# Attention over heads beside a layer of MLPs: how far ahead the MLPs run, and how the second halves of its tiles are issued

## The chip, the core and the metric

The kernel runs on one core of a Trainium2 chip. The core has five engines that take their instructions in program order, each from its own queue: TensorE (PE in the profile, with PEld for its weight loads), VectorE (DVE), ScalarE (ACT), GpSimd (POOL) and SyncE (SP, which issues most of the DMA transfers here). They wait for one another by semaphores. The metric is the device time of one execution in microseconds (us), and lower is better. The kernel before was timed six times: median 2488.54 us, from 2477.02 to 2491.85.

## The reference

Four transformer layers work on x, four sequences of 512 tokens and 288 channels, all float32. Each layer is attention and then an MLP, both with a normalisation, a shift and a scale ahead and a gate behind, which come from a conditioning vector per sequence. Layer 0's MLP is a mixture of four experts, two for each token. Layers 1 and 3 are plain. In layer 2 the attention runs over the 16 heads of one token, not over the tokens of a sequence:

```python
qkv = qkv.reshape(n, t, 3, H, DH)
q, k, v = (qkv[:, :, 0], qkv[:, :, 1], qkv[:, :, 2])
attn = jnp.einsum('nthd,ntkd->nthk', q * scale, k)
attn = jax.nn.softmax(attn, axis=-1)
out = jnp.einsum('nthk,ntkd->nthd', attn, v)
out = out.transpose(0, 2, 1, 3).reshape(n, t, d)
```

So each token has a 16 by 16 score matrix over vectors of 18, which the kernel computes on DVE and POOL, and the output is reshaped across tokens: a row of 288 channels that goes into the projection comes from many tokens of one head.

## The kernel before

The tokens are 16 tiles of 128, four for each of the four sequences (`B` = 4, `TB` = 4). The program is written out by a Python schedule. Time in it is counted in gaps: each piece of the main work on PE ends with a call of `gap(us)`, which may issue other work there. `gap` draws from four lists: `products` (work that needs PE and a PSUM bank), `lanes` (statistics and other work of DVE), `loads` and `spreads` (DMAs). An item has a due time in gaps and keys that must be ready; `mark(key, delay)` makes a key ready `delay` gaps later.

*Main work.* The attention of layer 1 runs in 64 steps of two gaps (`steps`, after 6 steps of lead). `INSIDE` names steps in the middle of which the whole MLP of one sequence of layer 1 is put (`early_mlp`, 512 tokens at a time); before, that is step 48, sequence 0. Six steps before the attention's end `begin_chain` starts the attention of layer 2, called the chain. Then come the other MLPs of layer 1 and those of layer 2 in halves of 256 tokens (`half_mlp`): two halves a sequence, 18 gaps a half. Each MLP of layer 2 waits, by a loop of empty gaps, until the normed rows of its sequence are ready (`ht`, 2, 1, b). Then layer 3's attention starts.

*The chain* (`attention_over_heads`). It is a generator, `stream`, which `follow` advances at each gap as far as a credit allows: every gap adds `flow["rate"]` (1.0 at first, then `RATE`), at most to 3.0, and each piece takes off the microseconds that it yields. Pieces that yield `BANK` need the one PSUM bank that a gap can give, and a `WAIT` ends a generator's turn until the next gap. A tile i goes through these steps:

- `kept(i, s)`: three products on PE for keys, values and queries (L839). Queries stay in one of two banks, the others are copied out by ACT (L848).
- `weigh(i, g)`, for four groups of four heads: a product (L857) and a sum (L863) on DVE give the scores `hs`.
- `shift(i)`: the maximum (L867) and its subtraction (L868), both on DVE. After every second tile ACT takes the Exp of two tiles (L1011).
- The second half, two tiles later: `denominators` (L889, DVE), `weighted(i, g)` on POOL (L873), `summed(i, g)` on DVE one tile later still (L885), `finish` (L897, POOL, and a DMA to scratch memory, L898).

The second half of an older tile is issued in the same loop as the first half of a newer one, `for i in range(n + 3)`, group by group.

*Beside the chain.* `beside` holds generators of two kinds for each sequence. `before(b)` normalises x for the chain. `after(b)`, started when a sequence's four tiles are finished, reads the reshaped rows back (`read`, L902), transposes (L915), projects (L922), adds to x, normalises and transposes again for the MLP of layer 2. They advance only while credit is above zero.

*Around it.* The weights of layer 3's attention (L248 to L257) are loaded by SP when the first products of layer 2's last sequence are done and the key "all spread" is marked; the chain marks it at its very end. SP issues in order, so a load that waits holds what stands behind it. Layer 1's and layer 2's MLP halves end with a copy on ACT (L1693) and two operations on POOL (L1694, L1695). In `gap`, products are issued early unless an item of the chain wants a bank.

## Time and profile before

One execution was profiled: 2483.05 us, of which the trace spans 2481.3 us; the mean granted TensorE clock is 0.943. The stages on PE, read from first and last instructions:

| stretch | from, us | to, us |
|---|---|---|
| one MLP of layer 1 inside its attention (L1596 to the last update) | 1232.2 | 1285.4 |
| first weigh of tile 0 to the last sum of tile 15 | 1366.7 | 1769.0 |
| first half MLP of layer 1 to the last half of layer 2 | 1366.7 | 1940.4 |
| attention of layer 3 and its MLPs | 1941.1 | 2481.3 |

| engine | busy over the span, us | share |
|---|---|---|
| PE | 2279.9 | 92% |
| DVE | 1087.0 | 44% |
| ACT | 833.0 | 34% |
| POOL | 528.3 | 21% |

The operations of the chain, by their rows:

| operation | engine, line | count | mean ns |
|---|---|---|---|
| product for the scores | DVE L857 | 64 | 1346 |
| sum over it | DVE L863 | 64 | 1353 |
| maximum | DVE L867 | 16 | 411 |
| subtraction | DVE L868 | 16 | 2089 |
| product with the values | POOL L873 | 64 | 3194 |
| sum over it | DVE L885 | 64 | 1332 |
| division by the denominator | POOL L897 | 16 | 759 |

A row of the slices is one engine over 40 equal parts of the span (62 us each), a digit being its busy share in tenths. In a row of the windows the stretch is followed by its length and then, for each engine, busy time and number of instructions, the granted clock, the share of the DMA engines and GB/s. In a row of a timeline the start and the length come first; the brackets at its end give the idle time of the engine before it and what ended it. For a line of code the least, median and largest duration in ns are given.

### The profile page before, as it was taken

The numbers are of one execution on the slowest core, as the hardware profiler recorded it, in microseconds if no ns is written. First come the engines' busy times: TensorE is split into PE (matmuls) and PEld (weight loads), VectorE is DVE, ScalarE is ACT, GpSimd is POOL, SyncE is SP. The second block draws the span as 40 slices with busy tenths as digits, with TensorE's granted clock in tenths as the row PEclk, the third lists the DMA queues.
The fourth block names the chain that finished last, engine by engine and source line by source line (L and its number), as shares of the span: only waits on it lengthen the run. The fifth ranks groups of instructions, "written<-read, shape, count | busy, mean of one in ns | idle before, by whom it ended". The sixth has DMA issues, their size and how long they took to land. (4 is left out here: it accounts for less than half of the span.)

```text
span 2481.3 us, 30149 instructions
## 1 busy us (share of the span) xinstructions
PE 2279.9 (92%) x11188; PEld 1210.4 (49%) x11188; DVE 1087.0 (44%) x1955; ACT 833.0 (34%) x1233; POOL 528.3 (21%) x544
## 2 busy tenths in 40 slices
PE   5999999799998999999999999778589999999998
PEld 2333333367775773333353677455456433333455
DVE  3556657240021025555424668989210455555100
ACT  1444444222221223344325233323223244444311
POOL 2000022120022111100010257778721100011000
PEclk8899999899999997899999899888799799999999
DMA  3311120355554541000000001100110000000000
GB/s 80 100 55 39 50 86 27 97 179 177 175 156 152 170 126 58 13 14 15 28 21 1 22 3 35 33 17 17 23 56 2 28 16 16 14 13 6 1 19 20
DMA packets 163033, 134.23 MB, mean 54 GB/s; under 512 B 81365, under 2 KB 146725, under 8 KB 162886
## 3 DMA queue, kind: packets, MB, share of 16 engines
q1 hardware_dynamic: 159520, 122.39, 16.9%
q0 software_dynamic: 3072, 9.44, 1.2%
q8 instruction: 89, 1.46, 0.2%
q14 instruction: 58, 0.48, 0.1%
q10 hardware_dynamic: 294, 0.47, 0.1%
HBM read 90.67 MB, written 26.25 MB: 47 GB/s over the span
## 5 line engine op out<-in xcount | busy, mean ns | idle before, releaser
L668 DVE TENSOR_REDUCE mx<-banks 128x1 f32<-128x512 f32 x696 | 448.2, 686 | 369.0 <-PE banks L616 367.2
L616 PE MATMUL banks<-qk 32*128 32x512 f32 x3072 | 542.8, 672 | 25.1 <-DMA qk<-qc 13.6
L661 ACT ACTIVATE ex<-banks 128x1024 f32<-128x1024 f32 x348 | 356.4, 1024 | 508.0 <-PE banks L616 499.9
L616 PEld LDWEIGHTS banks<-qk 32*128 32x128 f32 x3072 | 175.8, 191 | 240.0 <-DVE mx L668 95.3
L873 POOL TENSOR_TENSOR pv<-hs,qk 128x1152 f32<-128x1152 f32 x64 | 203.7, 3194 | 50.1 <-DVE ho L885 35.0
L690 PE MATMUL banks<-ex,va 128*32 128x512 f32 x1536 | 213.0, 626 | 0.0
L562 PE MATMUL banks<-ht,wqk 96*128 96x512 f32 (+1 forms) x360 | 189.7, 635 | 1.4 <-POOL wqk L284 0.8
L1472 PE MATMUL banks<-w_b,hid_b 128*128 128x288 f32 x684 | 189.5, 420 | 0.0
L1660 PE MATMUL banks<-ht,w 128*128 128x256 f32 x504 | 134.2, 401 | 38.4 <-ACT hid L1671 37.9
L1452 PE MATMUL banks<-block,w_b 128*128 128x256 f32 x684 | 165.4, 387 | 2.4 <-DMA w_b<-in_w 1.7
L710 POOL COPY rec<-r 128x512 f32<-128x512 f32 x48 | 29.6, 617 | 646.0 <-DVE r L706 572.3
L1464 ACT ACTIVATE hid_b<-banks,b_b 128x256 f32<-128x256 f32 x171 | 68.8, 473 | 246.1 <-PE banks L1458 144.3
L1682 PE MATMUL banks<-w,hid 128*128 128x288 f32 x504 | 151.4, 436 | 0.0
L1472 PEld LDWEIGHTS banks<-w_b,hid_b 128*128 128x128 f32 x684 | 125.1, 192 | 52.3 <-issue 24.4
L1452 PEld LDWEIGHTS banks<-block,w_b 128*128 128x128 f32 x684 | 129.4, 193 | 28.3 <-issue 8.2
L1660 PEld LDWEIGHTS banks<-ht,w 128*128 128x128 f32 x504 | 98.7, 201 | 62.0 <-ACT hid L1671 42.2
L727 PE MATMUL banks<-wp,ot 128*128 128x288 f32 x384 | 118.9, 435 | 5.9 <-DVE upd_a L522 3.5
L523 POOL TENSOR_TENSOR x<-x,upd_a 128x288 f32<-128x288 f32 x48 | 38.1, 794 | 364.2 <-DVE upd_a L522 341.6
L1682 PEld LDWEIGHTS banks<-w,hid 128*128 128x128 f32 x504 | 93.0, 197 | 45.8 <-issue 25.7
L562 PEld LDWEIGHTS banks<-ht,wqk 96*128 96x128 f32 (+1 forms) x360 | 61.6, 192 | 103.0 <-issue 89.1
L727 PEld LDWEIGHTS banks<-wp,ot 128*128 128x128 f32 x384 | 68.4, 194 | 75.2 <-issue 51.2
L690 PEld LDWEIGHTS banks<-ex,va 128*32 128x32 f32 x1536 | 31.1, 109 | 151.7 <-issue 149.9
(224 smaller groups left out, 2571.0 us busy)
## 6 DMA issues: line engine op xcount, KB each, us to landing
w_b<-in_w SPq DMA_DIRECT2D x57, 432.0 KB
w_b<-in_w SPq DMA_DIRECT2D x57, 384.0 KB
qk<-qc SPq DMA_DIRECT2D x327, 38.0 KB
wa<-in_wada SPq DMA_DIRECT2D x7, 864.0 KB
block<-x_mem SPq DMA_DIRECT2D x19, 288.0 KB
y_mem<-y_b SPq DMA_DIRECT2D x19, 288.0 KB
x_mem<-zeros SPq DMA_DIRECT2D x7, 768.0 KB
y_mem<-zeros SPq DMA_DIRECT2D x7, 768.0 KB
```

The costliest lines, as they stand in the source:

```text
L562: nc.tensor.matmul(to, st(rows, k), mv(rows, k), start=k == 0, stop=k == NK - 1)
L616: nc.tensor.matmul(to, qk[u][r, of, c * P : (c + 1) * P], qk[u][r, 1 - of, :], start=True, stop=True)
L661: nc.scalar.activation(e, WEIGHTS, AF.Exp)
L668: nc.vector.tensor_reduce(mxs[mu % 2][:, mc, h : h + 1], pm[j], AX.X, ALU.max)
L690: nc.tensor.matmul(SUMS[j * HP : (j + 1) * HP, :], vas[0][:, c, at : at + HP], ex[step, j // 2][:, j % 2, :], start=c == 0, stop=c == TB - 1,)
L727: nc.tensor.matmul(pp, done[b * NG + g][:, t * P : (t + 1) * P], w["wp"][:, g, :], start=g == 0, stop=g == NG - 1)
L873: nc.gpsimd.tensor_tensor(prod, sc[i][:, hs, :].unsqueeze(2).to_broadcast([P, GH, HD, NH]), qkv[i][:, 1].rearrange("p h d -> p d h").unsqu ...
L1452: nc.tensor.matmul(banks[:, UP + j, :BT], w1[:, k, j * P : (j + 1) * P], hx[i][:, k, :], start=k == 0, stop=False)
L1464: nc.scalar.activation(t, banks[:, UP + j, :BT], AF.Gelu_apprx_tanh, bias=b1[:, f : f + 1])
L1472: nc.tensor.matmul(banks[:, PY + t, :C], hid[j][:, t * P : (t + 1) * P], w2[:, j, :], start=f == 0, stop=f == NF - 1)
L1660: nc.tensor.matmul(banks[:, UP + j, :BT], full[:, k, (f % 3) * P : (f % 3 + 1) * P], h[:, k, s], start=k == 0, stop=False,)
L1682: nc.tensor.matmul(banks[:, PY + t, :C], hf[:, t * P : (t + 1) * P], w["w2"][f // 3][:, f % 3, :], start=False, stop=f == NF - 1,)
```

## The change

One more sequence's whole MLP of layer 1 is put inside its attention (steps 44 and 56, sequences 0 and 1), so four halves instead of six follow. `RATE` goes from 1.1 to 1.6. The subtraction of the maximum goes to POOL. The second halves are no longer issued by the tile loop's index but by their own counters (`at`): each weigh is followed by one `second()`, which issues one `weighted` and the `summed` that is two pieces behind; Exp for two tiles is issued one weigh into the tile after them. For the last two tiles every other `weighted`, and for the last tile the division, goes to DVE. Products for the next tile no longer hold the stream until they are possible. Items of `beside` that want a bank come first, and the others advance at least one piece a gap whatever the credit. The scores get four buffers instead of three; three empty gaps are put into the normalisations that ACT applies. The load of layer 3's attention weights no longer waits for the chain's end. Layer 2's MLPs also wait for their gate and count their due times anew. The normed rows behind the chain's projections may follow four gaps after them instead of six.

```diff
@@ -48,8 +48,8 @@
 N_BLOCKS = 2 * B * S // BT + NE - 1
-INSIDE = (48,)
-RATE = 1.1
+INSIDE = (44, 56)
+RATE = 1.6
 EARLY = 4
@@ -139,7 +139,7 @@
         before = flow["turn"]
-        wanted = any(item[1] for item in chain)
+        wanted = any(item[1] for item in chain + beside)
         fill(products, open_product, 0.0 if wanted else us)
@@ -172,12 +172,14 @@
-        for item in list(chain):
+        for item in beside + chain:
             if item[1]:
...
         for item in list(beside):
-            while flow["credit"] > 0 and piece(item):
-                pass
+            if not item[1]:
+                go_on = piece(item)
+                while go_on and flow["credit"] > 0:
+                    go_on = piece(item)
         for item in list(chain):
@@ -451,6 +453,8 @@
             nc.gpsimd.tensor_scalar_mul(off, off, -1.0)
+            for _ in range(3):
+                yield WAIT
         else:
@@ -778,7 +782,8 @@
         if l > 0:
-            task(loads, at_step(-LEAD) - 20, [("first products", prev, B - 1), ("all spread", prev)], load_attention(l))
+            spread_all = [] if prev == OVER_HEADS else [("all spread", prev)]
+            task(loads, at_step(-LEAD) - 20, [("first products", prev, B - 1)] + spread_all, load_attention(l))
             task(loads, at_step(-LEAD) - 20, [("x", prev, 1, B - 1)], load_projection(l))
@@ -852,7 +857,7 @@
             if g == 0:
-                sc[i] = work.tile([P, NH, NH], F32, tag="hs", bufs=3, name=f"hs_{l}_{i}")
+                sc[i] = work.tile([P, NH, NH], F32, tag="hs", bufs=4, name=f"hs_{l}_{i}")
             prod = work.tile([P, GH, NH, HD], F32, tag="va", bufs=1, name=f"pq_{l}_{i}_{g}")
@@ -865,12 +870,14 @@
             nc.vector.tensor_reduce(top, sc[i], AX.X, ALU.max)
-            nc.vector.tensor_tensor(sc[i], sc[i], top.to_broadcast([P, NH, NH]), ALU.subtract)
+            nc.gpsimd.tensor_tensor(sc[i], sc[i], top.to_broadcast([P, NH, NH]), ALU.subtract)
...
             prod = work.tile([P, GH, HD, NH], F32, tag="ex", bufs=4, name=f"pv_{l}_{i}_{g}")
-            nc.gpsimd.tensor_tensor(
+            engine = nc.vector if i >= len(tiles) - 2 and g % 2 else nc.gpsimd
+            engine.tensor_tensor(
                 prod,
@@ -894,7 +901,8 @@
             den = o.pop(("den", i))
-            nc.gpsimd.tensor_tensor(o[i], o[i], den.to_broadcast([P, NH, HD]), ALU.mult)
+            engine = nc.vector if i == len(tiles) - 1 else nc.gpsimd
+            engine.tensor_tensor(o[i], o[i], den.to_broadcast([P, NH, HD]), ALU.mult)
             nc.sync.dma_start(scratch[b][:, t * P : (t + 1) * P, :].rearrange("h t d -> t h d"), o[i])
@@ -963,7 +971,7 @@
                 yield -1.5
-            mark(("x", l, 1, b), 6)
+            mark(("x", l, 1, b), 4)
             yield from until(("x", l, 1, b))
@@ -979,41 +987,88 @@
             beside.append([before(1), False])
             yield from until(("values free", l - 1, B - 1, TB - 1))
             del ready["cleared"]
-            for i in range(n + 3):
+            at = {"shifted": 0, "weighed": 0, "weighted": 0, "summed": 0}
+            def second(behind=2):
+                k = at["weighted"]
+                cost = 0.0
+                if k < 4 * at["weighed"]:
+                    if k % 4 == 0:
+                        denominators(k // 4)
+                        cost += 0.7
+                    weighted(k // 4, k % 4)
+                    at["weighted"] += 1
+                k = at["summed"]
+                if k < at["weighted"] - behind:
+                    summed(k // 4, k % 4)
+                    at["summed"] += 1
+                    cost += 1.4
+                    if k % 4 == 3:
+                        finish(k // 4)
+                        if k // 4 % TB == TB - 1:
+                            beside.append([after(k // 4 // TB), False])
+                return cost
+            def exps():
+                for j in range(at["weighed"], at["weighed"] + 2):
+                    nc.scalar.activation(sc[j], sc[j], AF.Exp)
+                at["weighed"] += 2
+            def waiting():
+                return at["weighted"] < 4 * at["weighed"]
+            for i in range(n):
+                left = [1, 2, 0] if i + 1 < n else []
+                come = ("ht", l, 0, (i + 1) // TB)
+                def next_kept():
+                    s = left.pop(0)
+                    if s:
+                        yield BANK
+                    kept(i + 1, s)
+                    yield -1.5
                 for g in range(4):
-                    if i < n:
-                        weigh(i, g)
-                        yield 2.8
-                        if g > 0 and i + 1 < n:
-                            yield from until(("ht", l, 0, (i + 1) // TB))
-                            if g < 3:
-                                yield BANK
-                            kept(i + 1, g % 3)
-                            yield -1.5
-                    if g == 1 and 2 <= i < n + 2:
-                        denominators(i - 2)
-                        yield 0.7
-                    if i >= 3:
-                        summed(i - 3, g)
-                    if 2 <= i < n + 2:
-                        weighted(i - 2, g)
-                    yield 1.4 if i >= 3 else 0.0
-                if i >= 3:
-                    finish(i - 3)
-                    if (i - 3) % TB == TB - 1:
-                        beside.append([after((i - 3) // TB), False])
-                if i < n:
-                    shift(i)
-                    if i % TB == TB - 2:
-                        mark(("first products", l, i // TB), 1)
-                    if i % 2:
-                        for j in (i - 1, i):
-                            nc.scalar.activation(sc[j], sc[j], AF.Exp)
-                    yield 1.0
+                    weigh(i, g)
+                    yield 2.8
+                    if g > 0 and left and ready.get(come, 1 << 30) <= flow["now"]:
+                        yield from next_kept()
+                    if g == 1 and i % 2 == 0 and at["weighed"] < i:
+                        exps()
+                    if waiting():
+                        yield second()
+                shift(i)
+                if i % TB == TB - 2:
+                    mark(("first products", l, i // TB), 1)
+                at["shifted"] = i + 1
+                yield 0.4
                 if i % TB == 0 and 2 <= i // TB + 1 < B:
                     beside.append([before(i // TB + 1), False])
+                while left:
+                    if ready.get(come, 1 << 30) <= flow["now"]:
+                        yield from next_kept()
+                    elif waiting():
+                        second()
+                        yield 3.2
+                    elif at["weighed"] + 2 <= at["shifted"]:
+                        for _ in range(4):
+                            yield WAIT
+                        exps()
+                    elif at["summed"] < at["weighted"]:
+                        yield second(0)
+                    else:
+                        yield WAIT
+            while at["summed"] < 4 * n:
+                if not waiting() and at["weighed"] < n:
+                    yield WAIT
+                    yield WAIT
+                    exps()
+                second(2 if waiting() else 0)
+                yield 2.8
             mark(("over heads", l))
-            mark(("all spread", l))
             yield from clear()
         return stream()
@@ -1133,7 +1188,7 @@
                 arenas.append(
-                    work.tile([P, NH, NH], F32, tag="hs", bufs=3, name=f"arena{len(arenas)}").rearrange("p a b -> p (a b)")
+                    work.tile([P, NH, NH], F32, tag="hs", bufs=4, name=f"arena{len(arenas)}").rearrange("p a b -> p (a b)")
                 )
@@ -1832,8 +1887,9 @@
     for b in range(B):
-        while ready.get(("ht", 2, 1, b), 1 << 30) > flow["now"]:
+        while any(ready.get(key, 1 << 30) > flow["now"] for key in (("ht", 2, 1, b), ("gate", 2, 1))):
             gap(0.5)
+        rebase(starts["mlp", 2] + 2 * b * MLP_GAPS)
         for half in range(2):
...
     flush(2)
```

## The prediction

> **What bounds the kernel now.** I read the page's slices first: PE is at nine tenths almost everywhere, and falls away in one stretch alone, slices 25 to 29 (1550 to 1860 us), where DVE and POOL are the busy ones. The page's groups, the table of 20 us windows and one line's durations carry the rest.
>
> Page, busy tenths in 40 slices of 62 us:
> ```profile
> PE   5999999799998999999999999778589999999998
> DVE  3556657240021025555424668989210455555100
> POOL 2000022120022111100010257778721100011000
> PEclk8899999899999997899999899888799799999999
> ```
> Windows, engine by engine (PE, PEld, DVE, ACT, POOL), then the granted clock:
> ```profile
> 1524.00:1544.00 20.00, 20.00 (x93) 14.92 (x91) 19.49 (x16) 6.23 (x13) 15.04 (x8) 1.00 0.29 60
> 1584.00:1604.00 20.00, 11.56 (x37) 8.41 (x38) 17.98 (x19) 7.80 (x14) 18.21 (x14) 0.78 0.00 0
> 1624.00:1644.00 20.00, 7.91 (x37) 5.16 (x35) 19.17 (x16) 5.02 (x8) 14.76 (x8) 0.81 0.17 37
> 1784.00:1804.00 20.00, 2.39 (x15) 1.76 (x12) 0.00 (x0) 1.55 (x2) 4.41 (x12) 0.65 0.43 73
> 1884.00:1904.00 20.00, 20.00 (x90) 14.18 (x89) 1.17 (x4) 4.47 (x10) 2.81 (x3) 1.00 0.00 1
> ```
> The stage runs from 1366.7 us (first weigh of tile 0) to 1941.1 (first score of the last attention). DVE is full from about 1484 to 1720, PE full from 1804 on, and in two places neither is: 1436 to 1455 and 1769 to 1804. The timelines of DVE, PE and the SP queue name those two:
> ```profile
> 1454.91 0.46 DVE L442 BATCH_NORM_STATS2 st<-x 128x6 f32<-128x288 f32 x1 [18.55 <-POOL x L1695]
> ```
> ```profile
> 1804.69 1.06 PE L915 MATMUL banks<-ident,rows 128*96 128x128 f32 x4 [18.31 <-DMA rows<-scratch]
> ```
> ```profile
> 1777.77 1.99 SPq L248 DMA_DIRECT2D wqk<-in_wqk  x3
> ...
> 1799.85 0.63 SPq L252 DMA_DIRECT2D wqk<-in_bqk  x1
> 1800.58 0.40 SPq L902 DMA_DIRECT2D rows<-scratch  x1
> ```
> In the first, DVE stands in order behind statistics of an x that the MLP of sequence 1 has not finished. In the second, the rows of the last sequence are issued behind a train of weight loads 22.8 us long (1777.8 to 1800.6), and PE stands behind the rows. The lines of the subtraction and of a product beside it (least, median, largest ns):
> ```profile
> L868 DVE TENSOR_TENSOR hs<-hs,ht x16: 424/2536/3324, 1389.7 to 1730.4; 128x256 f32<-128x256 f32 x16
> ```
> ```profile
> L857 DVE TENSOR_TENSOR pq<-banks,qk x64: 1294/1348/1359, 1366.7 to 1726.0; 128x1152 f32<-128x1152 f32 x64
> ```
> A subtraction of 0.42 us takes up to 3.3, about one POOL product (3.19).
>
> **The change, part by part.** *One more whole MLP ahead of the chain.* Whole MLPs of the last layer end 37.2 us apart (2366.4, 2403.6, 2440.8). After the one inside attention 1 PE idles 3.7 us, so I take 37.2 + 3.7 = 41 us of later start; ends are 37 and the 53 us that the present one lasts (1232.2 to 1285.4, other products among it). First weigh: 1366.7 + 41 = 1408. This is paid in full, as PE is busy 0.92 to 0.98 there (1116 to 1364). The two halves that it replaces leave the stage behind.
>
> *Stall at sequence 1.* Its x is now complete before the chain starts, so the 18.6 us and the 4.3 us for the next product go. Sequence 2 is late next: its MLP is 36 gaps of the first half stage, and DVE then needs it only at tile 8. Price nothing, cover four tiles of DVE.
>
> *Subtraction.* 16 x 2.09 = 33.4 us leave DVE; POOL gets 16 x about 0.68 (its 288 element product, least 0.67) = 11. Queued behind it on POOL are the products of older tiles, behind its result the two Exp on ACT, behind these the Gelu of the MLP; Exp is now issued one weigh or more later, which covers about 4 us. Starts of tiles 7 to 15 (1537.07 to 1711.38) are 21.8 us apart, and the subtractions in them average 2.4, so the period becomes 19.4 us. DVE's own rows give 4 x (1.35 + 1.35 + 1.33) + 0.41 + 0.41 + 0.25 = 17.2, with 8 x 0.62 / 4 = 1.24 of statistics 18.5: that is the lower end, 21.8 the upper (nothing gained), and I take 19.4 because its rows are of the same stretch. The fourth hs buffer removes waits of L863 for POOL, 9.1 us in five times; I leave them inside those ends.
>
> *Rate 1.6 and second halves on their own count.* A tile is worth 4 x 2.8 + 4 x 1.4 + 0.7 + 1.0 - 3 x 1.5 = 14.0 of credit now, 12.7 gaps at 1.1; after, 13.4 at 1.6, 8.4 gaps. A half MLP is 18 gaps and 20 to 22.6 us of PE (copies at 1876.6, 1899.0, 1921.8, 1940.4), so a tile carries 8.4 x 1.15 + 4.4 (its 18 products) = 14 us of PE work, some 3 more with transposes and projections: less than 19.4, so DVE keeps setting the pace and PE does less beside it than now. POOL has 4 x 3.19 + 0.76 + 0.68 + about 4 of updates = 18, close.
>
> *Chain end.* Tiles 0 and 1 have no second halves: 48.3 us now, 44 at the higher rate. Then 14 x 19.4 = 272. Weigh of tile 15 ends at 1408 + 44 + 272 = 1724 (1729 now). The tail is now 35 us (1733.7 to 1769.0), POOL products with DVE waiting. Nine second halves stay, four of the last eight products on DVE, 2.8 of credit each: 16 gaps, 20 us (ends 12 and 35). A product on DVE has no row; it lies between 1.35 (L857) and 1.35 + 3.2 (if it waits as L868 did), and I take 2.9, the middle, inside the 20. Last sum 1744, against 1769.
>
> *Handover.* The weights of the last attention no longer wait for the chain, so their train comes right after tile 14. The 18.3 us before the last rows go. But SP is in order: by count, the rows of sequence 2 are issued within one gap of the train. If the train is first, PE stands at those rows instead, up to 18.3 us; if not, nothing. I take the middle, 9. The scratch writes behind it have two tiles (39 us) of cover.
>
> *PE after the chain.* Waiting: statistics and transposes that want a bank now move each gap, not only on credit. Tile 3 is done at tile 6.6, 48 gaps after the start; about 37 more to its normed rows, 85; the four halves of layer 1 end at 72, so 13 gaps without an MLP. The new wait for the gate is covered: its row needs the end of layer 1, gap 77, and four products, 81. The chain has some 128 gaps, so 43 go to layer 2, 2.4 halves; 5.6 remain, against 4.6 at 1804.7. Now 1804.7 to 1941.1 is 136.4 us; one half more is 20: 156. The stage ends at 1744 + 9 + 156 = 1909, against 1941: 32 us. Norm's three new waits (3 gaps, 1.2 us each) are in the 37; sorting of the beside list costs nothing, it only orders issues. The 540 us behind the stage stay. The profiled execution took 2483.05 (span 2481.3): 2451. It lies 5.5 under the median of the six runs (2488.54), so 2457.
>
> **A rule against one step.** L868 reads two tensors in SBUF and waits, L857 reads one from PSUM and never does; L873 stretches only from 3.12 to 3.42. The Trainium skill, GPSIMD Engine Reference, Specifications, says that POOL's SBUF interfaces are shared with DVE and contended by DVE instructions with two SBUF inputs, which agrees with both lines; its Perfetto Trace Analysis, Optimizing Scalar/DVE Operations, warns that for this reason moving work between the two might not help. By the warning the subtraction gives nothing: that is a rival below.
>
> **Rivals.**
> *A. As worked out*, 2457, own range 2435 to 2478. Chance 0.48.
> *B. The ends fall well*: period 18.5 (13 us), train behind the rows (9), tail 12 (8), half an MLP fewer left (10): 40 more, 2417. For it: DVE is 95% busy at 21.8 us a tile, so nothing else holds it. Against: POOL at 18 of 18.5. Chance 0.20.
> *C. Period stays 21.8*, POOL or its port bounding: 14 x 2.4 = 34 us, 2491. For it: POOL is 18.2 of 20 busy at 1584. Against: there DVE is the one it waits for (L885, 35 us). Chance 0.14. The quoted warning ends here.
> *D. Slower: Exp behind the pool's queue.* ACT waited for the subtraction up to 14.3 us, and the Gelu and PE behind it. Should that come at each of the seven pairs, half of it on DVE's path through late products, 50 us: 2507. It decides from about 5.5 us a pair (32 / 5.5, six or seven pairs). For it: one more engine between maximum and Exp. Against: Exp is issued later than now. Chance 0.18.
>
> **Numbers.** 0.3% (7.5 us) is about what can be told from no change. Faster by more: A, B and a fifth of C, 0.71; within: most of C, 0.09; slower: D and a little of C, 0.20. The range takes B's end and C's, leaving most of D out: 2413 to 2500.
>
> **What would show it.** First weigh near 1408; no L442 wait of 18 us; subtractions on POOL under 1 us; tile starts 19.4 apart (21.8 would be C); last sum near 1744; PE's idle before L915 short, or 18 us at sequence 2; five to six upd_m copies after the chain; last attention at 1909. Wrong if tiles keep their period, or if PE still waits tens of us for the normed rows of layer 2.

## The result, and the profile after

The changed kernel takes 2471.91 us (median; 2467.11 to 2482.0), beside 2485.01 for the kernel before in the same runs: a ratio of 0.9948, 95% interval 0.9936 to 0.996. That is a gain of 0.52%, some 13 us, where the forecast had 31.5. The profiled execution took 2469.37 us (span 2467.3).

All of the comparison below goes by the stage from the first weigh of tile 0 to the first score of the last attention. The earlier layers shift its start by up to 14 us from one execution to another without any edit to them (1390.2 to 1404.7 us among the versions below with two whole MLPs ahead), so its length is the sharper reading; the ratios beside it are of whole executions. The kernel before was timed again beside each batch of experiments (medians 2477.8 to 2486.9 us), so two runs are compared by their ratios to it and not by their times.

| point | before, us | forecast | after, us |
|---|---|---|---|
| first weigh of tile 0 | 1366.7 | 1408 | 1402.4 |
| maximum of tile 15 (end of its weighing) | 1729.9 | 1724 | 1730.2 |
| last sum of tile 15 | 1769.0 | 1744 | 1801.0 |
| from there to the first score of the last attention | 172.1 | 165 | 126.6 |
| first score of the last attention | 1941.1 | 1909 | 1927.6 |
| length of the stage | 574.4 | 501 | 525.2 |

The page's slices of the kernel after, busy tenths in 40 slices of 61.7 us:

```profile
PE   5999999799998999999999898897689999999998
DVE  3455656331021015555343389669420455555100
POOL 2000022121022011100010149769441000001000
PEclk8899999899999997999999998898789799999999
```

The hole of PE is narrower than before, and it is deepest at 7 and 6, in slices 27 and 28, about 1666 to 1789 us. Three windows of the kernel after (PE, PEld, DVE, ACT, POOL; granted clock; DMA share; GB/s) show two different stretches of the chain:

```profile
1480.00:1500.00 20.00, 18.69 (x80) 13.43 (x79) 19.79 (x19) 6.42 (x13) 19.73 (x10) 1.00 0.07 7
1704.00:1724.00 20.00, 10.23 (x24) 6.31 (x24) 19.72 (x22) 3.47 (x8) 16.14 (x13) 0.59 0.26 27
1724.00:1744.00 20.00, 1.42 (x5) 1.04 (x6) 7.84 (x7) 0.30 (x1) 5.31 (x6) 0.50 0.49 70
```

In the first, DVE and POOL are both full and PE almost: what the change was read to do. In the last, little computes: PE is busy 1.4 of 20 us, DVE 7.8, and the granted clock is 0.50. PE's timeline and the SP queue's name it:

```profile
1742.58 1.09 PE L923 MATMUL banks<-ident,rows 128*96 128x128 f32 x4 [28.09 <-DMA rows<-scratch]
```
```profile
1714.46 0.36 SPq L906 DMA_DIRECT2D scratch<-ho  x1
1714.91 1.98 SPq L250 DMA_DIRECT2D wqk<-in_wqk  x3
...
1737.39 0.63 SPq L254 DMA_DIRECT2D wqk<-in_bqk  x1
1738.06 0.46 SPq L910 DMA_DIRECT2D rows<-scratch  x1
```

PE comes to the transposes of sequence 2 at 1742.58 - 28.09 = 1714.5, just as the last scratch write of that sequence is issued (1714.46). Then SP issues the last attention's weight train, 23.2 us, and only at 1738.06 the read of the rows, which PE can use 4.5 us later. PE waits out the whole of it. Behind PE stand ACT and then DVE, in their own order:

```profile
1743.70 0.58 ACT L924 COPY rt<-banks 96x512 f32<-96x512 f32 x1 [30.13 <-PE banks L923]
```
```profile
1767.26 0.42 DVE L896 TENSOR_REDUCE hd<-hs 128x16 f32<-128x256 f32 x1 [35.38 <-ACT hs L1017]
```

ACT's copies for the transposed and projected rows are in front of the Exp of the last two tiles, so the second halves of those tiles begin 35 us late, and the tail is 70.8 us long (40.7 in a version below in which nothing stands at the rows). POOL, where the subtraction of tile 15 now is, stands in the same way:

```profile
1752.06 0.79 POOL L935 TENSOR_TENSOR upd_a<-upd_a,gate 128x288 f32<-128x288 f32 x1 [22.67 <-ACT upd_a L934]
...
1756.81 0.62 POOL L873 TENSOR_TENSOR hs<-hs,ht 128x256 f32<-128x256 f32 x1
```

Its maximum was there at 1730.6; the subtraction waits 26 us behind an update that waits for the rows. The duration of the subtraction is about as forecast, 0.62 us where 0.68 was taken (least, median, largest ns):

```profile
L873 POOL TENSOR_TENSOR hs<-hs,ht x16: 613/622/642, 1425.5 to 1756.8; 128x256 f32<-128x256 f32 x16
```

Over the stage, before and then after:

```profile
1366.70:1941.10 574.40, 491.53 (x2037) 344.25 (x2037) 331.24 (x376) 169.46 (x323) 310.21 (x221) 0.90 0.12 25
```
```profile
1402.40:1927.60 525.20, 445.69 (x1835) 311.74 (x1833) 310.27 (x357) 156.45 (x297) 297.86 (x223) 0.89 0.13 28
```

PE idles 574.4 - 491.5 = 83 us before and 525.2 - 445.7 = 79.5 after. The stage is 49 us shorter almost only by the work that was moved ahead of it (36 us of later start pay for that); the idle time that the change was to fill has stayed.

### The profile page after: what moved, and what is told of

Same layout as the page of the kernel before. It is cut to its first block, busy times and chain, and to the rows that moved or that the text cites. A ratio compares the mean times of both kernels' runs of the same rounds, so it can differ in the third digit from the quotient of the medians.

```text
span 2467.3 us, 30012 instructions
## 1 busy us (share of the span) xinstructions
PE 2266.4 (92%) x11134; PEld 1197.2 (49%) x11134; DVE 1069.2 (43%) x1946; ACT 832.8 (34%) x1225; POOL 520.0 (21%) x553
## 4 chain that ended last, share of the span: by engine, by line
PE 76%; DVE 8%; POOL 4%; DMA 4%; issue 2%; ACT 2%; SPq 2%; another core or an unknown queue 0%; ACTq 0%; POOLq 0%; DVEq 0%
PE banks L620 19%; PE banks L566 10%; PE banks L694 7%; PE banks L1527 7%; PE banks L1507 6%; PE banks L731 4%; PE banks L1678 4%; PE banks L1651 4%; POOL pv L880 3%; PE banks L1737 2%; PE banks L1715 2%; PE banks L1513 1%; DVE pq L862 1%; DVE mx L672 1%; DVE ho L892 1%
## 5 line engine op out<-in xcount | busy, mean ns | idle before, releaser
L620 PE MATMUL banks<-qk 32*128 32x512 f32 x3072 | 533.2, 670 | 24.8 <-DMA qk<-qc 13.5
L880 POOL TENSOR_TENSOR pv<-hs,qk 128x1152 f32<-128x1152 f32 x60 | 190.4, 3187 | 22.9 <-ACT hs L1017 22.8
L1715 PE MATMUL banks<-ht,w 128*128 128x256 f32 x432 | 117.1, 406 | 13.9 <-ACT hid L1726 13.9
L1737 PE MATMUL banks<-w,hid 128*128 128x288 f32 x432 | 128.6, 434 | 0.0
L1678 PE MATMUL banks<-w,hid 128*128 128x288 f32 x432 | 109.1, 410 | 0.0
L1715 PEld LDWEIGHTS banks<-ht,w 128*128 128x128 f32 x432 | 86.3, 205 | 33.7 <-ACT hid L1726 17.5
```

Source lines behind the costliest of these rows:

```text
L620: nc.tensor.matmul(to, qk[u][r, of, c * P : (c + 1) * P], qk[u][r, 1 - of, :], start=True, stop=True)
L880: engine.tensor_tensor(prod, sc[i][:, hs, :].unsqueeze(2).to_broadcast([P, GH, HD, NH]), qkv[i][:, 1].rearrange("p h d -> p d h").unsqueez ...
L1678: nc.tensor.matmul(banks[:, t, :C], hf[:, t * P : (t + 1) * P], w["w2"][f // 3][:, f % 3, :], start=False, stop=f == NF - 1,)
L1715: nc.tensor.matmul(banks[:, UP + j, :BT], full[:, k, (f % 3) * P : (f % 3 + 1) * P], h[:, k, s], start=k == 0, stop=False,)
L1737: nc.tensor.matmul(banks[:, PY + t, :C], hf[:, t * P : (t + 1) * P], w["w2"][f // 3][:, f % 3, :], start=False, stop=f == NF - 1,)
```

## The experiments

The theory: the idle time is at the rows. Two things put it there: the weight train ahead of the rows of sequence 2, and the three empty gaps between a read and its transposes, which PE is through before the read has landed. The rivals: the higher rate or the new order of the second halves holds the chain; the division of work between DVE and POOL does; the products at the end of the chain do. Where nothing else is said an edit is made to the kernel after.

### The train, moved

The load of the last attention waits until the rows of sequence 2 have been read:

```diff
-spread_all = [] if prev == OVER_HEADS else [("all spread", prev)]
+spread_all = [("rows read", prev, 2)] if prev == OVER_HEADS else [("all spread", prev)]
             read(b)
+            mark(("rows read", l, b), 0)
```

> The changed kernel, but the train of weight loads for the last attention is issued only once the rows of sequence 2 are issued (one added key), so it stands behind them and ahead of the rows of sequence 3. Theory T (the missing gain is the 28.1 us in which PE stands at the rows of sequence 2, priced at 9 in the prediction): PE's wait there falls to the 5 to 7 us that sequences 0 and 1 show, the Exp of the last two tiles is no longer 35 us late, and the time falls from 2472 by 19 to 28 us, to 2444 to 2453. Rival R (the stand is covered, PE being full from 1824 us on with work that only waits for the MLPs' order): under 5 us, 2467 to 2472.

Measured: 2451.89 us, ratio 0.9896 (0.9866 to 0.9925); stage 517.0 us. The kernel after is at 0.9948, so the move gives 0.52%, 13 us, less than the 19 to 28 of theory T, and the stage is 8 us shorter. PE's timeline of this kernel has what is left of the stand, and the SP queue's why:

```profile
1716.12 1.09 PE L923 MATMUL banks<-ident,rows 128*96 128x128 f32 x4 [11.14 <-DMA rows<-scratch]
```
```profile
1705.03 0.36 SPq L906 DMA_DIRECT2D scratch<-ho  x1
1711.76 0.36 SPq L910 DMA_DIRECT2D rows<-scratch  x1
1712.18 1.54 SPq L250 DMA_DIRECT2D wqk<-in_wqk  x3
```

The train is now behind the read, and still PE stands 11.1 us, where T had 5 to 7; at sequence 0 it stands 8.8 in this execution. The write to scratch memory (1705.03) must land before the read is issued, 6.7 us later; the rows are there after another 4.4. A round trip of 11 us is what the gaps were to cover (three ahead of the read and three behind it), and at this sequence PE was through all of them when the write was issued. The sums over the stage say the same, the kernel after and then this one (total, times, longest):

```profile
PE banks L923 <- DMA rows<-scratch: 40.0, 3, 28.1
```
```profile
PE banks L923 <- DMA rows<-scratch: 25.8, 3, 11.1
```

### The train, one sequence later

The same edit with sequence 3 in place of 2.

> The changed kernel with the train issued only behind the rows of sequence 3, the last. T: as the run before, 2444 to 2453, unless the last attention's first products now wait for their weights, which would show as idle time of PE ahead of L566 after 1800 us. R: 2467 to 2472.

Measured: 2460.51 us, ratio 0.9928 (0.99 to 0.9956), stage 520.4. The stand at sequence 2 is the same (11.0), and the last sequence adds one of 13.0 us. The time is in neither forecast's range, and by the ratio the version can't be told from the one above; nothing speaks for holding the train longer.

### The train, back at the chain's end

The edit of the load is undone: "all spread" is marked at the end of the chain and waited for again.

> The changed kernel with this one edit undone: the train waits for the chain's end again, and the mark is back there. T: the stand moves from sequence 2 to sequence 3; there it was 18.3 us before the change, and the chain is not held by it, so about half of the 28 us comes back: 2455 to 2465. R: 2467 to 2472.

Measured: 2478.37 us, ratio 0.9996 (0.9978 to 1.0013), stage 537.6: slower than the kernel after by 0.48%, 12 us, and no faster than the kernel before. Both forecasts missed it: T had half of the 28 us coming back. The chain does end sooner (its tail is 54 us in place of 70.8), but a stand of the same size is now at the last sequence, behind the chain:

```profile
1806.34 1.09 PE L923 MATMUL banks<-ident,rows 128*96 128x128 f32 x4 [29.56 <-DMA rows<-scratch]
```

So the load's earlier place is worth 12 us as it stands, though it only moves a stand of 28 to 30 us from one sequence to another: in this version PE still stands 10.7 us at sequence 2, without the train.

### Nine gaps in place of three

The train stays where the change has it; what moves is the distance from a read to its transposes:

```diff
             read(b)
-            for _ in range(3):
+            for _ in range(9):
                 yield WAIT
```

> After, with nine empty gaps instead of three between the read of a sequence's rows and their transposes; the train of weight loads stays where it is, ahead of the rows of sequence 2. Theory (the train delays the rows of sequence 2 by 22.8 us and the distance to their use covers only three gaps, some 10 us with the issue): nine gaps are 11 to 15 us of PE work more or less, so the stand at the rows of sequence 2 falls from 28.1 to 10 to 17 us and the short ones (6.5, 5.4) vanish; stage from first weigh to first score 495 to 512 us (after: 525; both edits together: 480), time 2440 to 2458. Rival (the distance alone does it, the train is without effect): stand under 3 us, stage within 5 us of 480, time 2425. Second rival (the train alone does it): stand over 22 us, stage over 517.

Measured: 2437.86 us, ratio 0.9816 (0.979 to 0.9841), stage 491.2: a further 1.3%, 33 us, better than the kernel after. The stand at sequence 2 is 10.4 us and the two short ones are gone, as the theory had it; stage and time are a few us better than its lower ends.

```profile
1719.97 1.09 PE L923 MATMUL banks<-ident,rows 128*96 128x128 f32 x4 [10.35 <-DMA rows<-scratch]
```

Six gaps took 17.7 us off the long stand and all of the 12 us of the short ones, 30 in all, out of a stage that is 34 us shorter. They also change the order of PE's work. In the kernel after, the transposes of sequence 0's rows (1538.59) and its four projections are issued ahead of the products of tile 8, the first of sequence 2, and DVE waits for these. With more gaps the same products come ahead of the transposes (1543.49). PE and DVE in the kernel after, then PE in the version of the next section, which has nine gaps too:

```profile
1555.59 1.62 PE L930 MATMUL banks<-wp,rt 96*128 96x288 f32 x6
1557.92 1.62 PE L844 MATMUL banks<-wqk,ht 96*128 96x288 f32 x6
1564.36 1.36 DVE L862 TENSOR_TENSOR pq<-banks,qk 128x1152 f32<-128x1152 f32 x1 [18.30 <-PE banks L844]
```
```profile
1538.29 3.08 PE L844 MATMUL banks<-wqk,ht 96*128 96x288 f32 x12
```

DVE's waits for the products of tiles 8 and 12, 18.3 and 10.9 us, are gone with nine gaps and still there (19.1 and 12.5) with the train moved alone. So the 33 us are the worth of the gaps, and how much of them is the landing of the rows and how much the order was not separated.

### Both

> The train behind the rows of sequence 2, and nine empty gaps instead of three between the issue of a sequence's rows and the first transpose that reads them. Theory T2 (what is left of the stand is PE, which is in order, meeting transposes issued too few gaps after their DMA; at rate 1.6 three gaps are about 4 us and the rows take 6 to 11 more): PE's waits at L923, 25.8 + 6.1 us with the train moved alone, fall under 5, and the stage (first weigh to first score of the last attention, 517.0 us with the train moved alone, 525.2 in the changed kernel) to about 490 to 500. Rival (the waits are only PE's slack, since layer 2's MLPs cannot start earlier anyway): stage 510 or more.

Measured: 2424.95 us, ratio 0.9752 (0.9727 to 0.9777), stage 479.5, shorter than theory T2 had. It is 2.0% below the kernel after (some 49 us), about the sum of the two edits (13 + 33). No transpose waits for rows. The windows of this kernel over the same minutes of the chain as above:

```profile
1480.00:1500.00 20.00, 18.67 (x80) 13.41 (x80) 19.79 (x18) 6.61 (x12) 19.70 (x9) 1.00 0.07 8
1704.00:1724.00 20.00, 19.42 (x82) 14.33 (x80) 16.17 (x16) 7.69 (x14) 19.84 (x13) 0.88 0.39 51
1724.00:1744.00 20.00, 15.37 (x59) 10.96 (x60) 10.29 (x9) 5.10 (x10) 19.69 (x13) 0.83 0.07 7
```

At 1480 nothing has changed; at 1704 to 1744 PE has 34.8 us of work in place of 11.7. The tail from the maximum of tile 15 to the last sum is 40.7 us in place of 70.8. Over the whole stage:

```profile
1404.66:1884.18 479.52, 435.24 (x1836) 305.36 (x1834) 304.22 (x357) 156.03 (x297) 303.50 (x223) 0.93 0.14 30
```

PE's idle time is 44.3 us, from 79.5; and its busy time falls too, by 10.5 us for the same instructions, at a granted clock of 0.93 in place of 0.89.

### Both, in the kernel before

The same two edits, and nothing of the change:

```diff
-[("first products", prev, B - 1), ("all spread", prev)], load_attention(l))
+[("first products", prev, B - 1), ("rows read", prev, 2) if prev == OVER_HEADS else ("all spread", prev)], load_attention(l))
             read(b)
-            for _ in range(3):
+            mark(("rows read", l, b), 0)
+            for _ in range(9):
                 yield WAIT
```

> The kernel before, none of the change in it, with the last attention's loads behind the read of the rows of sequence 2 and nine empty gaps after each read. Theory (before, the chain's end is set by DVE at 21.8 us a tile and the two stands at its ends; of these the one of 18.3 us at the rows of the last sequence goes, the one of 18.6 us at sequence 1 stays): stage from 574 to 545 to 562 us, time 2462 to 2478, 10 to 23 us under before. Rival (the read and the train are all that there was to gain, the rest of the change gives nothing by itself): as good as the version with both in after, 2425 to 2435. Second rival (no gain, as another wait of the last sequence takes the place): within 5 us of before.

Measured: 2469.34 us, ratio 0.9927 (0.9898 to 0.9957), stage 557.3: 18 us better than before, as the theory had it. Here the train was the only obstacle at the rows: in the kernel before, PE comes to the transposes of sequences 0 to 2 only 22.8, 21.7 and 9.7 us after the last write, with the same three gaps, and does not stand there. The stand at the last sequence's rows is gone, and the one at sequence 1's statistics, which the change removes, is still there:

```profile
1456.60 0.46 DVE L442 BATCH_NORM_STATS2 st<-x 128x6 f32<-128x288 f32 x1 [18.53 <-POOL x L1696]
```

This makes a square. Without the two edits the change is worth 0.5%; with them it is worth 0.9752 / 0.9927 = 0.982, 1.8%, some 44 us. So the change with the rows mended is worth more than the 31.5 us forecast, and some 31 us of it were given back in what the two edits mend.

### The subtraction, back on DVE

```diff
-nc.gpsimd.tensor_tensor(sc[i], sc[i], top.to_broadcast([P, NH, NH]), ALU.subtract)
+nc.vector.tensor_tensor(sc[i], sc[i], top.to_broadcast([P, NH, NH]), ALU.subtract)
```

> The changed kernel with the subtraction on DVE again. By the prediction's price (2.4 us a tile, 14 tiles, DVE setting the pace) 34 us slower, 2506. By what the changed profile shows (unblocked tiles 16.5 us apart, and DVE idle 18.3, 10.9 and 35.4 us behind PE) the stage is no longer set by DVE's sum: 0 to 12 us slower, 2472 to 2484.

Measured: 2486.67 us, ratio 1.0033 (1.0016 to 1.005), stage 547.8: slower than the kernel after by 0.85%, 21 us, which is between the two forecasts (34, and 0 to 12). The row of this kernel (least, median, largest ns):

```profile
L873 DVE TENSOR_TENSOR hs<-hs,ht x16: 424/1225/3403, 1423.7 to 1746.3; 128x256 f32<-128x256 f32 x16
```

Sixteen of them take 24.1 us of DVE (mean 1509 ns), and the tiles come 21.8 us apart (maxima of tiles 1 to 15), against 20.6 in the kernel after. The stand at the rows of sequence 2 is there as well, 28.5 us, and the tail behind it, 71.8 us from the maximum of tile 15: so the two causes are apart, and the tail is no work of the subtraction on POOL. In the chain as the change orders it, the move to POOL is a gain.

### The subtraction, on POOL in the kernel before

The same one line, the other way, in the kernel before.

> The kernel before with one edit, the subtraction of the maximum on POOL. Theory (DVE sets the pace of the tiles there, and 33 us of subtraction leave it): tiles 7 to 15 from 21.8 to 19 to 20.5 us apart, last sum 20 to 30 us earlier after first weigh than 402 us, of which 10 to 25 us reach the end, as PE then does less beside the chain: time 2460 to 2475. Rival (Exp is issued right behind the tile there, so it waits on ACT for POOL's queue and the Gelu behind it): Exp waits over 5 us a pair, time same or slower, 2482 to 2500.

Measured: 2489.24 us, ratio 1.0004 (0.9988 to 1.002), stage 578.7: no difference. DVE is relieved, and the tiles do not come closer: maxima of tiles 7 to 15 are 22.4 us apart, and 22.1 before. In the stretch of tiles 7 to 15, before and then with the edit:

```profile
1537.00:1711.40 174.40, 139.66 (x557) 98.42 (x558) 158.41 (x162) 53.86 (x100) 135.07 (x82) 0.85 0.13 24
```
```profile
1538.50:1711.50 173.00, 136.23 (x535) 96.07 (x535) 139.54 (x154) 51.86 (x97) 136.77 (x89) 0.84 0.13 24
```

DVE's busy time falls from 158.4 to 139.5 us, and waits take the place. DVE's waits from 1500 to 1730, before and then with the edit:

```profile
DVE hs L863 <- POOL pv L873: 9.1, 5, 2.4
DVE pq L857 <- PE banks L839: 7.8, 4, 4.0
```
```profile
DVE pq L857 <- PE banks L839: 26.6, 6, 8.3
DVE hs L863 <- POOL pv L873: 17.6, 7, 4.9
```

The products of the next tile come no sooner, and the three score buffers come free no sooner. The Exp of the pairs waits somewhat longer for the subtraction, 32.7 us in all against 22.3; the rival's time came, and its mechanism in a small part. The theory was wrong here: DVE was 91% busy in that stretch (rival B of the prediction has 95%), and it did not set the pace alone. The rate of 1.1 makes a tile 12.7 gaps (the prediction's count), and 22 us is 1.7 us a gap; that the schedule's credit is the second thing at the same pace is argued from this, not shown.

### Fewer MLPs ahead, the old rate, the last products on POOL

Three single parts of the change, each undone alone: `INSIDE = (48,)`; `RATE = 1.1`; and every product with the values on POOL (`engine = nc.gpsimd` in `weighted`).

> The changed kernel with one whole MLP inside the attention again, at step 48. By the prediction's prices the stage starts 41 us earlier and carries two halves (40 to 45 us) more, and DVE stands again behind sequence 1 (18.6 + 4.3 us): 15 to 25 us slower, ratio about 1.002 to 1.006 to the kernel before. Rival (PE idles 78 us in the stage, which the two halves would fill): 10 to 20 us faster than the changed kernel, 0.987 to 0.991.

> The changed kernel at rate 1.1. If DVE sets the pace (the prediction), a slower issue only puts more PE work beside each tile, and the time stays within 10 us: 0.992 to 0.998. If PE sets it wherever both are busy (DVE waits for L844 31.3 us and for Exp 46.6 us in the changed profile), 12.2 gaps a tile make about 21 us of PE work instead of 17, the chain ends some 50 us later, and the last sequence's MLP with it: 1.000 to 1.012.

> The changed kernel with all products of the last two tiles on POOL. On DVE they take 3.96 us each, longer than POOL's 3.19. The prediction counted the tail at 20 us with them and up to 35 without: 12 to 15 us slower. If the tail waits for Exp and PE (35.4 us of DVE's idle time there), not for the products: within 5 us of the changed kernel, 0.993 to 0.997.

| undone | us | ratio to before | stage |
|---|---|---|---|
| nothing (kernel after) | 2471.91 | 0.9948 (0.9936 to 0.996) | 525.2 |
| two whole MLPs ahead | 2476.77 | 0.9968 (0.9951 to 0.9984) | 568.4 |
| rate 1.6 | 2465.89 | 0.9928 (0.9906 to 0.995) | 520.5 |
| last products on DVE | 2470.44 | 0.9945 (0.9926 to 0.9963) | 525.4 |

The intervals of all three overlap with that of the kernel after. One MLP ahead starts the chain 35 us sooner and makes the stage 43 us longer. Its time lies between the two forecasts, 0.2% (5 us) above the kernel after, at the edge of what can be told: as long as the stands are there, the second whole MLP ahead, with its two halves less, gains little by itself. In this version DVE stands at the fifth tile, the first of sequence 1, for its products: the stall that the change removes, one tile further on and longer (timeline of DVE in that kernel):

```profile
1509.75 1.36 DVE L862 TENSOR_TENSOR pq<-banks,qk 128x1152 f32<-128x1152 f32 x1 [31.82 <-PE banks L844]
```

At the rate of 1.1 the time stays where the first forecast had it, and PE still stands at the rows of all four sequences (4.2, 2.7, 22.5 and 4.3 us). The products of the last two tiles are not what the tail waits for, as the second forecast of that run had it.

### The lower rate, with both edits

The version with the train moved and nine gaps, its rate 1.2 in place of 1.6.

> The version with the train behind the rows of sequence 2 and nine empty gaps, its rate set from 1.6 to 1.2. Theory (DVE and POOL are full in the middle of the chain, 19.7 of 20 us at 1460 to 1500 each, so the credit is not what spaces the tiles, but at the two gaps it decides how much MLP work lies beside a tile): tiles 1 to 2 us further apart, last sum 10 to 25 us later after first weigh than 349 us, less PE idle beside the chain and less PE work left after it; stage 475 to 490 us, time within 8 us of 2425. Rival (the higher rate is what makes the gain, since the chain's length sets the end): last sum over 25 us later and stage over 495, time over 2440.

Measured: 2423.41 us, ratio 0.9742 (0.9719 to 0.9766), stage 476.2: the same as at 1.6 within the intervals. The last sum comes 356 us after the first weigh, 7 us later than at 1.6, and PE has less left behind it. The tiles are hardly further apart (19.4 us on the mean, 19.2 at 1.6); both shifts are less than the theory had. One stand of 3.3 us is left, at the rows of sequence 2. The rate, once the long stands are gone, moves a little work from one side of the chain's end to the other. These two versions are the fastest of this study, 2.5% below the kernel before.

## Why the prediction was right and wrong

The direction was right and the time lies in the range given; the gain was forecast at 31.5 us and is 13. That the time is in the range is in part luck: two terms missed in opposite directions, the tail by 51 us too short and the work behind the chain by 38 us too long. Step by step:

- **One more MLP ahead.** 41 us were forecast, 35.7 measured between the two profiles. Right, within the shift between executions.
- **The stall at sequence 1.** Gone, as said. The edit that undoes it has its successor at 31.8 us. But "sequence 2 is late next" was priced at nothing, and DVE waits 18.3 us at its first tile, tile 8, and 10.9 at tile 12, the first of sequence 3. Not a late MLP holds tile 8: the transposes of its normed rows are on PE at 1527.9 to 1531. Its products come behind the transposes and projections of sequence 0.
- **Subtraction.** 0.62 us on POOL, where 0.68 was taken. Sixteen leave DVE, and undoing this costs 21 us. The Trainium skill's Perfetto Trace Analysis, Optimizing Scalar/DVE Operations, warned that moving work between these two might not help. In the kernel after the measurement decides against the warning (0.85%). In the kernel before the move alone gave nothing (1.0004), but there new waits for products and buffers took the place, and POOL's product kept its median (3.19 us without the move, 3.18 with it).
- **Period.** 19.4 us were forecast with DVE as the pace. Undisturbed tiles are 16.5 to 18.8 us apart in the kernel after (maxima of tiles 1 to 7, 1442.0 to 1545.7), most of them under the lower end of 18.5. That end was a sum of durations, and neighbouring rows of DVE overlap a little: 17.2 us of them fit into the 16.5 from the maximum of tile 3 (1477.3) to the next (1493.8). But the next eight are 23.1 apart, no less than before (22.1), since three long waits are among them (gaps of 37, 25 and 32 us between maxima; DVE waits 18.3 and 10.9 us for products and 7.6 for Exp). The mean over 14 tiles is 20.6; with both edits it is 19.2. The error of this term against the forecast is 14 x 1.2 = 17 us; 10 of it were made good by a start 5.6 us earlier and two first tiles 4.4 us shorter, so weighing ended at 1730 where 1724 was forecast.
- **Tail.** 20 us forecast, 70.8 measured, 40.7 with the stands removed. So 30 of the 51 us missed belong to the two steps below. The other 20 are a mis-sized term: 16 gaps in 20 us are 1.25 us a gap, and with the stands removed it is twice that, if the count of 16 holds. Why was not tried on its own.
- **Handover: the step that failed.** The train was seen, its length (22.8 us) and its place before the rows of sequence 2 were seen; the price was put between nothing and 18.3, and 9 was taken. It measured 28.1. The upper end was taken from a stand in which PE had come (1786.4) when 8.6 us of the train were already out. The right bound was in the same lines of the profile before: the train, 22.8, and from the issue of the rows (1800.58) to their first transpose (1804.69) another 4.1, so 27 us for a PE that comes when the train starts. And the step priced PE's wait alone and added it behind the last sum; it came at 1714 to 1742, ahead of the second halves of the last two tiles, and ACT's copy behind it (30.1) and Exp behind that (DVE 35.4) put it into the chain's tail.
- **PE after the chain, waiting.** The three gaps between a read and its transposes were among "about 37" and taken as covering. In the kernel before they did cover the trip through scratch memory, 10 to 11 us: PE came to the transposes of sequences 0 to 2 at 22.8, 21.7 and 9.7 us after the end of the last write's issue. In the kernel after it comes 3.1 and 3.8 us after it at sequences 0 and 1, and 0.3 us before it at sequence 2. The prediction saw that this work now moves at each gap and not only on credit, and counted that as a gain alone. The lower rate does not bring the distance back (4.5 to 7.0 us at 1.1, all else as in the kernel after); that the rule of one piece a gap is what took it fits the code, and was not tried alone. It cost 12 us at sequences 0 and 1, which no term held, and it is what made the train's stand 28 rather than 10. With nine gaps the kernel gains 33 us, with the train moved as well 49. From the last sum to the last attention 165 us were forecast and 126.6 measured, because PE did part of that work while the chain's end was late.
- **The rivals.** Rival D, Exp behind the pool's queue, did not come pair by pair: ACT waited 3.8 us in all for the subtractions on POOL. At the last pair a subtraction did sit 26 us in that queue, but ACT's own copies came later still, and with the subtraction back on DVE the tail is as long. C, a period that stays, came in its number over tiles 7 to 15 (23.1 us, 22.1 before) and not in its cause: undisturbed tiles are 16.5 to 18.8 apart, and the three long gaps are waits for PE and ACT. With both edits tiles 7 to 15 are 20.7 apart, and POOL is 19.7 of 20 us busy at 1480, as full as DVE; that it sets the pace there together with DVE is not excluded. B's first half (a shorter period) came with both edits only in part (19.2), and its second (the train behind the rows) was what the experiment had to make: that version ends at 2425, near B's 2417.

What stays open: which part of the change brought PE to the rows so early, and how the 33 us of the nine gaps divide between the landing of the rows and the order of PE's work. The new order of the second halves, the order and the rule of the list `beside`, the fourth score buffer and the shorter delay of the mark were not tried alone.

## What to carry to other kernels

A load that is freed of a wait goes out at once, and on a queue that issues in order everything behind it is late by its whole issue time (23.2 us here); price that as the full train plus the landing of what stands behind it, for an engine that arrives as the train starts, and then follow the stand to the next engines' queues. A distance counted in schedule slots between a write and a read through memory must be held against the measured round trip each time the schedule is made denser: here the same three slots were enough before the change and not after it, and six more were worth 33 us, where the subtraction that the change moved was worth 21. And an engine that is 91% busy need not be the pace: relieving it in the kernel before gave nothing, and two other waits took the place.

## What the runs showed of the hardware

A stand has a second cost. The four transposes right behind a wait take 1.06 to 1.09 us in the kernel after, and the same four take 0.60 in the version in which none waits (kernel after, then the version with both edits, timelines of PE):

```profile
1538.59 1.06 PE L923 MATMUL banks<-ident,rows 128*96 128x128 f32 x4 [6.52 <-DMA rows<-scratch]
1542.81 1.06 PE L923 MATMUL banks<-ident,rows 128*96 128x128 f32 x4
```
```profile
1543.49 0.60 PE L923 MATMUL banks<-ident,rows 128*96 128x128 f32 x4
```

A stand of 6.5 us is enough, the second group is still slow 4 us later, and the granted clock from 1536.0 to 1546.2 is 0.50. Stands of 2.3 us (one whole MLP ahead) and 2.7 us (rate 1.1) left the transposes at 0.62 and 0.64; one of 3.3 us (both edits at rate 1.2) was followed by 1.09. Over the stage PE's busy time fell by 10.5 us with the stands removed, for the same instructions: about a quarter of the 45.7 us by which the stage became shorter. The Trainium skill, TensorE: Matmul & The Clock Gate, "Why this matters for your kernels", advises against idle gaps of PE over some 3 us, since one idle window sets the clock back to half. The granted clock of 0.50 from 1724 to 1744, the 1.06 against 0.60 and the three short stands agree.

Second, the product with the values that the change gives to DVE takes 2.1 to 4.8 us (median 4.5) in the kernel after, while the same engine's product for the scores, as many elements with one input in PSUM, takes 1.35. What POOL is doing when the product starts makes the difference. Here it starts 0.9 us into one of POOL's own products, and then with none running:

```profile
1768.19 3.16 POOL L880 TENSOR_TENSOR pv<-hs,qk 128x1152 f32<-128x1152 f32 x1
1769.10 4.26 DVE L880 TENSOR_TENSOR pv<-hs,qk 128x1152 f32<-128x1152 f32 x1
```
```profile
1785.74 2.10 DVE L880 TENSOR_TENSOR pv<-hs,qk 128x1152 f32<-128x1152 f32 x1
```

In the first case it ends 2.0 us after POOL's product, and so do the other two long ones: about 2 us of work behind a wait for POOL. In the second case POOL waits instead: its multiplication at 1785.81 (L455), begun 0.07 us after DVE's product, takes 2.15 us, and the same line takes 0.23 at its other five places in the chain. With both edits the four products take 2.1 to 2.5 us, since none starts early in a POOL product, and there POOL's updates of 0.79 us that begin just behind take 2.6 and 2.7. So in these overlaps the instruction that starts second waits for the first, and POOL's products keep their 3.19 because they come first. What in the chip makes them wait was not tried here.
